# Moving the attention's weighted values one step later, next to the scores of another step

## The chip, the cores and the metric

The kernel runs on one core of a Trainium2 chip. The metric is the device time of one execution in microseconds. Five engines work at the same time, each on its own queue of instructions: PE (TensorE, matrix multiplies and transposes), DVE (VectorE), ACT (ScalarE), POOL (GpSimd) and SP (SyncE, which issues most of the DMAs). Instructions of different engines wait for each other on semaphores. PE writes its results to PSUM, which has eight banks; the other engines work mostly from SBUF.

## What is computed

Two layers run over a tensor x of 8 images, 256 channels and 64 x 64 points, all in float32. Layer 0 is an involution: 1x1 convolutions produce values and, through a small network, nine weights for each point and group of channels; each point gets the weighted sum of its nine neighbours. Layer 1 adds an attention over 7 x 7 neighbourhoods to a depthwise double convolution with weights computed at run time. The part that the change touches is the attention of layer 1:

```
att = einsum('bdn,bdkn->bnk', q, uk + upe[None])      # scores of a point against its 49 neighbours
att = softmax(att, axis=-1)                            # probabilities
out_att = einsum('bnk,bdkn->bdn', att, uv)             # weighted values
...
return rate1 * out_att + rate2 * out_conv
```

Both layers are residual: x = x + layer(groupnorm(x)).

## The kernel before

An image is cut into 8 bands of 8 rows; the 64 bands of layer 1 are numbered g, with b the image and i the band in it. One band of layer 1 takes 8 steps: `ct` (which 128 of the 256 channels, two heads of 64) times `m` (which 16 of the 64 columns). Layer 0 of a band 12 bands ahead runs beside layer 1, a piece in each step; in the last image nothing of layer 0 is left to run.

The order of the work on every engine is the order in which the program is written. A step is written out by hand in six parts, each of which ends with `advance()`. This call also runs whatever was put off by `after(n, f)`, n parts later. In a step of layer 1, in this order:

1. `scores` (L682): four matmuls of 64 x 64 tiles against 196 columns into the score tile `sco` (L692), a 14 x 14 window of keys for each of two 8 x 8 tiles of queries and two heads. VectorE adds the mask, writes the result to `prob`, and takes the negated maximum `nmax` of each row (L701). `transposed` (L720): PE transposes the probabilities of the step before (L724, tile `ptp`), and ScalarE copies them to SBUF as `pt` (L726). `exponentials`: ScalarE, with the row sums in `tot` (L709).
2. `branch_weights`: PE computes 512 columns of the convolution's dynamic weights (L814, tile `pf`), ScalarE takes their exponential into `ex` (L819). Two taps of the depthwise convolution on VectorE (L771 or L797).
3. `probabilities`: VectorE inverts `tot` (L716), ScalarE scales by it (L718). Then the work listed by `beside` for this step: queries (L625, copied out by ScalarE at L629), keys (L646, finished by VectorE at L654 and L661), values (L551), pieces of layer 0.
4. `weighted_values` (L729): eight products of `pt` with the values `vt` (L736, up to 112 rows, 64 columns of weights, 64 columns streamed), for the step before. They go to an unused part of the same score tile that this step's scores have filled. `add_values` (L744): VectorE adds the result to `xr`, the residual that is stored at the end of the band (L746). Then the remaining taps of this half.
5. The second `branch_weights` of the step; at the end of each `ct` the sum over the branches, on POOL and VectorE (`dynamic_sum`, L825 to L844).
6. More of the work beside: tap weights of layer 0 (L435, tile `pw`). VectorE multiplies them with the values (L448, tile `prod`) and POOL adds the products up (L456, tile `xg`), parts later.

PSUM is divided as follows. The score tile takes two banks and there is one such tile. So the scores of a step wait until VectorE has finished with everything in the tile of the step before. All other PE results (`pf`, `ptp`, `pw`, queries, keys, values) share five banks under the tag "gen". The accumulator of the depthwise convolution takes the last bank. In SBUF there are three `prob` tiles, two `pt` tiles and nine `vt` tiles.

Of the kernel before, what the change touches and what calls it, by code (L numbers as in the profile page):

```python
# [86 lines left out]
def conv_layers_kernel(ctx: ExitStack, tc: tile.TileContext, ins: dict, out: bass.AP):  # L87
# [98 lines left out]
    def layer1_loads():  # L186


        last = w1.tile([P, NCT, 1, C], F32, tag="rec", name="last", bufs=1)
        for f in late:  # L190
            f()
        nc.scalar.dma_start(out=last, in_=wfc_in[:, :, KK - 1 :])

        def first():
            nc.vector.tensor_scalar(wv, wv, rate1, None, ALU.mult)

        def difference(kt):
            nc.vector.tensor_sub(wfc[:, kt], wfc[:, kt], last[:, kt].to_broadcast([P, KK - 1, C]))  # L200

        return [first, lambda: difference(0), lambda: difference(1)]
# [12 lines left out]
    def after(n, f):  # L215
        later.append((place[0] + n, f))

    def advance():
        place[0] += 1
        ready = [f for p, f in later if p <= place[0]]  # L220
        later[:] = [d for d in later if d[0] > place[0]]
        for f in ready:
            f()
# [51 lines left out]
    def first_stats(b, i, use="xs", t=None, n=9):  # L275
        im = images[b]
        if i == 0:
            im.st0 = stat.tile([P, NCT, NB, 6], F32, tag="st", name=f"st0_{b}")
        x = load_x(b, i, use, t)

        def take():
            for ct in range(NCT):
                nc.vector.bn_stats(im.st0[:, ct, i, :], x[:, ct, :])

        after(n, take)
        return x
# [391 lines left out]
    def score_tile(nm):  # L678

        return ps.tile([P, 2, 512], F32, tag="sco", name=f"sco_{nm}")  # L680

    def scores(b, i, ct, m):  # L682


        im = images[b]
        qb, kb = im.qb[i, ct], im.kb[i, ct]
        nm = f"{b}_{i}_{ct}_{m}"
        sco = score_tile(nm)
        for t in range(2):
            for h in range(2):  # L690
                c0 = (2 * m + t) * TQ
                nc.tensor.matmul(  # L692
                    sco[half[t], h, :NKEY], qb[half[h], 2 * m + t].rearrange("p r c -> p (r c)"),
                    kb[half[h], :, c0 : c0 + KW], start=True, stop=True,
                )

        prob = probs[turn[0] % len(probs)]
        turn[0] += 1
        nmax = w1.tile([P, 2], F32, tag="nmax", name=f"nmax_{nm}", bufs=4)
        for h in range(2):  # L700
            nc.vector.tensor_tensor_reduce(  # L701
                prob[:, h, :NKEY], sco[:, h, :NKEY], mask, -1.0, 3.0e38, ALU.add, ALU.min, nmax[:, h : h + 1]
            )
        return sco, prob, nmax

    def exponentials(nm, prob, nmax):
        tot = w1.tile([P, 2], F32, tag="tot", name=f"tot_{nm}", bufs=4)
        for h in range(2):
            nc.scalar.activation(  # L709
                prob[:, h, :NKEY], prob[:, h, :NKEY], AF.Exp, bias=nmax[:, h : h + 1], scale=-1.0,  # L710
                accum_out=tot[:, h : h + 1],
            )
        return tot
# [6 lines left out]
    def transposed(nm, prob):  # L720
        ptp = ps.tile([CHUNK, 2, 2, P], F32, tag="gen", name=f"ptp_{nm}", bufs=5)
        for h in range(2):
            for ch in range(2):
                nc.tensor.transpose(ptp[:, h, ch], prob[:, h, ch * CHUNK : (ch + 1) * CHUNK], ident)  # L724
        pt = w1.tile([CHUNK, 2, 2, P], F32, tag="pt", name=f"pt_{nm}")
        nc.scalar.copy(pt, ptp)  # L726
        return pt

    def weighted_values(b, i, ct, m, pt, sco):  # L729
        im = images[b]  # L730
        po = sco[:, 0, 256 : 256 + 2 * NQ].rearrange("p (r c) -> p r c", r=R)
        for t in range(2):
            for ch in range(2):
                n = min(R, WP - (i + ch) * R) * KW
                for h in range(2):
                    nc.tensor.matmul(  # L736
                        po[half[h], :, t * TQ : (t + 1) * TQ],
                        im.vt[i + ch, m][:n, t, (2 * ct + h) * HD : (2 * ct + h + 1) * HD],
                        pt[:n, h, ch, t * NQ : (t + 1) * NQ],
                        start=(ch == 0), stop=(ch == 1),  # L740
                    )
        return po

    def add_values(b, i, ct, m, po):  # L744
        x = images[b].xr[i][:, ct].rearrange("p (r c) -> p r c", r=R)[:, :, 2 * m * TQ : 2 * (m + 1) * TQ]
        nc.vector.scalar_tensor_tensor(x, po, bv[:, ct : ct + 1], x, ALU.add, ALU.add)  # L746
# [203 lines left out]
    with tc.manual_schedule():  # L950

        for i, use in enumerate(("xc", "xc", "xr", "xr", "xs", None, None, None)):
            t = None
            if use is None:
                t = w1.tile([P, NCT, RP, W], F32, tag="yp", name=f"x_{i}", bufs=3)
                t = t.rearrange("p t r c -> p t (r c)")[:, :, :BAND]
            x = first_stats(0, i, use, t)
            if use == "xc":
                images[0].xc[i] = x
            advance()  # L960
        for r in range(NB, AHEAD0 - AHEAD):
            first_stats(*divmod(r, NB))
        for _ in range(10):
            advance()
        scaled_weights(0)
        for _ in range(32):
            advance()
        for n, f in enumerate(layer1_loads()):
            after(4 * STEPS * (3 + n), f)
        before = conv = None  # L970
        for g in range(-AHEAD, B * NB):
            b, i = divmod(g, NB)
            for s in range(STEPS):
                ct, m = divmod(s, NT // 2)
                mid, end = beside(g, s)
                steer(g, s)
                if g >= 0:
                    nm = f"{b}_{i}_{ct}_{m}"
                    sco, prob, nmax = scores(b, i, ct, m)
                    if before is not None:  # L980
                        pt = transposed(nm, before[-1])
                    tot = exponentials(nm, prob, nmax)
                advance()
                if g >= 0:
                    ex, exb = w1.tile([P, 2, BAND], F32, tag="ex", name=f"ex_{nm}", bufs=3), ex if m else None
                    branch_weights(b, i, ct, m, 0, ex)
                    if m in (0, 2):
                        todo = list(conv[0])
                    for _ in range(2):
                        todo.pop(0)()  # L990
                advance()
                if g >= 0:
                    probabilities(prob, tot)
                rest = [f() for f in mid]
                advance()
                if g >= 0:
                    if before is not None:
                        add_values(*before[:-1], weighted_values(*before[:-1], pt, sco))
                for f in rest:
                    if f:  # L1000
                        f()
                if g >= 0:
                    for _ in range(2 if m % 2 == 0 else len(todo)):
                        todo.pop(0)()
                    before = (b, i, ct, m, prob)
                advance()
                if g >= 0:
                    branch_weights(b, i, ct, m, 1, ex)
                    if exb is not None:
                        after(4, lambda ex=ex, exb=exb: nc.gpsimd.tensor_add(ex, ex, exb))  # L1010
                    if m == 1:
                        conv[1]()
                        conv = depthwise_middle(b, i, ct)
                    if m == NT // 2 - 1:
                        oc = depthwise_end(b, i, ct, conv[1])
                        after(4, lambda a=(b, i, ct, ex, oc): dynamic_sum(*a))
                if s % 4 == 3 and 0 <= (g * NCT + ct + 1) < B * NB * NCT:
                    gn, cn = divmod(g * NCT + ct + 1, NCT)
                    conv = depthwise_begin(*divmod(gn, NB), cn)
                advance()  # L1020
                for f in end:
                    f()
                advance()
        sco = score_tile("end")
        add_values(*before[:-1], weighted_values(*before[:-1], transposed("end", before[-1]), sco))
        for _ in range(40):
            advance()

# [81 lines left out]
```

The softmax here doesn't subtract the row's maximum and nothing guards it: scores larger than these inputs give would overflow.

## Time and profile before

| | before |
|---|---|
| time, median of 3 runs | 4332.86 us (4330.35 to 4334.35) |
| profiled span | 4333.4 us |
| start, before the first scores of layer 1 | 257.3 us |
| granted TensorE clock | 0.992 of full speed |
| scores L692, on PE | 4096 matmuls, mean 357 ns |
| weighted values L736, on PE | 8176 matmuls, mean 228 ns |
| additions L746, on VectorE | 511, mean 343 ns |
| dynamic weights L814, on PE | 4096 matmuls, mean 607 ns |

A float32 product appears in the trace as two matmuls. The duration of a matmul covers its way through the array, and consecutive ones overlap; what one costs the engine is therefore read from the distance between two starts, not from its duration. Small matmuls on different parts of the array run at the same time. In the profile "X <- Y" is an engine that sat idle ahead of its instruction X until Y released it, followed by the sum in microseconds, the number of times and the longest time. PEld is the weight load of TensorE, which overlaps matmuls.

### The profile page before, as it was taken

The page shows a single profiled execution, that of the slowest core. Times are in us where ns is not written, and L with a number is a line of the kernel's source. Part 1 is how long each engine was busy: PE and PEld are TensorE (multiplying, and loading weights), DVE is VectorE, ACT ScalarE, POOL GpSimd, SP SyncE. Part 2 cuts the span into 40 slices and gives each one's busy share as a digit, 9 for nine tenths or more (in the row PEclk, how much of TensorE's full clock was granted, in tenths as well). Part 3 has the DMA queues.
Part 4 walks back from the last instruction along what each step waited for, and adds up shares of the span by engine and source line. Part 5 has one row for each costly group of instructions (what it writes and reads, how often), then busy time and mean ns, then how long its engine had stood idle before and what let it go on. Part 6 is the DMA issues. An engine that isn't in the chain of part 4 may idle for free.

```text
span 4333.4 us, 72039 instructions
## 1 busy us (share of the span) xinstructions
PE 4174.8 (96%) x25004; PEld 2104.1 (49%) x25004; DVE 3577.6 (83%) x7244; ACT 3059.9 (71%) x7598; POOL 2900.3 (67%) x1778
## 2 busy tenths in 40 slices
PE   6789999999999999999999999999999999999998
PEld 3344445444454444544455444554445444454444
DVE  5778888888888888888888888888888888977777
ACT  3367777777777777877777777777677777677776
POOL 4657677676776767767776767766776777744445
PEclk9899999999999999999999999999999999999999
DMA  7754234234233333333333333343332232111100
GB/s 214 188 130 106 69 87 105 69 91 100 64 97 96 79 89 87 84 91 95 76 84 95 82 95 84 75 101 83 77 88 78 66 96 73 35 44 37 37 27 20
DMA packets 381259, 367.90 MB, mean 85 GB/s; under 512 B 55392, under 2 KB 282720, under 8 KB 380640
## 3 DMA queue, kind: packets, MB, share of 16 engines
q1 hardware_dynamic: 377568, 358.68, 32.6%
q8 instruction: 198, 3.24, 0.3%
q10 hardware_dynamic: 3328, 4.62, 0.3%
q14 instruction: 165, 1.35, 0.1%
HBM read 261.48 MB, written 101.71 MB: 84 GB/s over the span
## 4 chain that ended last, share of the span: by engine, by line
PE 61%; DVE 19%; POOL 11%; issue 5%; SPq 1%; DMA 1%; ACT 1%; POOLq 0%; ACTq 0%; DVEq 0%
PE pf L814 27%; POOL xg L456 6%; PE sco L736 5%; PE p L357 4%; PE pk L646 4%; DVE prod L448 4%; PE ptp L724 4%; PE sco L692 4%; DVE acc L771 3%; POOL ex L1010 3%; PE pq L625 3%; PE pvt L595 3%; DVE ex L832 2%; PE p L325 2%; DVE acc L797 2%
## 5 line engine op out<-in xcount | busy, mean ns | idle before, releaser
L814 PE MATMUL pf<-yp,c_wfc 128*128 128x512 f32 x4096 | 1985.1, 607 | 0.9
L456 POOL TENSOR_TENSOR xg<-xg,prod 128x1024 f32<-128x1024 f32 x549 | 1204.1, 2193 | 131.6 <-DVE prod L448 109.8
L1010 POOL TENSOR_TENSOR ex<-ex,ex 128x1024 f32<-128x1024 f32 x384 | 907.8, 2364 | 76.0 <-ACT ex L819 71.3
L814 PEld LDWEIGHTS pf<-yp,c_wfc 128*128 128x128 f32 x4096 | 696.2, 190 | 535.1 <-issue 491.0
L819 ACT ACTIVATE ex<-pf 128x512 f32<-128x512 f32 x1024 | 608.4, 594 | 453.6 <-PE pf L814 263.5
L842 POOL TENSOR_TENSOR ex<-ex,rec 128x512 f32<-128x512 f32 x128 | 163.7, 1279 | 1006.7 <-DVE rec L837 946.6
L771 DVE SCALAR_TENSOR_TENSOR acc<-yp,c_chan,acc 128x504 f32<-128x504 f32 (+3 forms) x1104 | 765.1, 693 | 55.4 <-ACT acc L762 35.0
L797 DVE SCALAR_TENSOR_TENSOR acc<-hid,c_chan,acc 128x504 f32<-128x504 f32 (+3 forms) x1024 | 758.0, 740 | 18.6 <-ACT acc L791 0.6
L448 DVE SCALAR_TENSOR_TENSOR prod<-pw,c_par,x3q 128x1040 f32<-128x1040 f32 x576 | 733.8, 1280 | 33.6 <-POOL xg L456 19.4
L718 ACT ACTIVATE prob<-prob,tot 128x196 f32<-128x196 f32 x1024 | 411.6, 451 | 427.6 <-DVE tot L716 427.6
L709 ACT ACTIVATE prob<-prob,nmax 128x196 f32<-128x196 f32 x1024 | 461.7, 455 | 85.7 <-DVE nmax L701 85.3
L736 PEld LDWEIGHTS sco<-pt,vt 112*64 112x64 f32 x8176 | 281.5, 137 | 363.5 <-issue 139.7
L701 DVE CUSTOM_DVE_ANT_0 prob<-sco,c_mask 128x196 f32<-128x196 f32 x1024 | 324.5, 355 | 159.8 <-PE sco L692 159.6
L746 DVE SCALAR_TENSOR_TENSOR xr<-sco,bv,xr 128x128 f32<-128x128 f32 x511 | 175.4, 343 | 334.5 <-PE sco L736 334.5
L736 PE MATMUL sco<-pt,vt 112*64 112x64 f32 x8176 | 350.2, 228 | 30.3 <-DVE nmax L701 28.4
L724 PE MATMUL ptp<-ident,prob 128*112 128x128 f32 x2044 | 331.6, 285 | 0.0
L726 ACT COPY pt<-ptp 112x512 f32<-112x512 f32 x511 | 296.3, 580 | 39.4 <-PE ptp L724 39.3
L692 PE MATMUL sco<-kb,qb 64*64 64x196 f32 x4096 | 294.7, 357 | 24.5 <-DVE xr L746 24.5
L724 PEld LDWEIGHTS ptp<-ident,prob 128*112 128x112 f32 x2044 | 206.4, 133 | 152.0 <-issue 66.0
L551 PE MATMUL pv<-yp,c_wv 128*128 128x512 f32 (+2 forms) x576 | 251.9, 562 | 0.0
L646 PE MATMUL pk<-yp,c_wk 128*128 128x512 f32 (+2 forms) x576 | 244.9, 552 | 0.0
L357 PE MATMUL p<-xc,w3s 128*128 128x512 f32 x512 | 243.7, 599 | 0.0
(133 smaller groups left out, 5359.2 us busy)
## 6 DMA issues: line engine op xcount, KB each, us to landing
x<-x3n SPq DMA_DIRECT2D x128, 264.0 KB, 2.1
x3q<-x SPq DMA_DIRECT2D x128, 264.0 KB, 7.1
xc<-in_x SPq DMA_DIRECT2D x64, 512.0 KB, 5.1
xg<-in_x SPq DMA_DIRECT2D x256, 128.0 KB, 4.8
x<-xg SPq DMA_DIRECT2D x256, 128.0 KB, 2.4
yp<-x SPq DMA_DIRECT2D x128, 256.0 KB, 3.3
xr<-x SPq DMA_DIRECT2D x64, 512.0 KB, 5.8
out_x<-xr SPq DMA_DIRECT2D x64, 512.0 KB, 3.1
```

The lines of the kernel that those rows point to most:

```text
L448: nc.vector.scalar_tensor_tensor(prod[:, :, :RUN], pw[:, j, :RUN].unsqueeze(1).to_broadcast([P, SHARE, RUN]), par[:, PCB2 + k : PCB2 + k + 1],
L456: nc.gpsimd.tensor_add(im.xg[i], im.xg[i], rows(prod))
L646: nc.tensor.matmul(pk[:, :n], wk[:, kt, ct * P : (ct + 1) * P], im.yp[i][:, kt, a : a + n], start=(kt == 0), stop=(kt == NCT - 1),)
L692: nc.tensor.matmul(sco[half[t], h, :NKEY], qb[half[h], 2 * m + t].rearrange("p r c -> p (r c)"), kb[half[h], :, c0 : c0 + KW], start=True, ...
L709: nc.scalar.activation(prob[:, h, :NKEY], prob[:, h, :NKEY], AF.Exp, bias=nmax[:, h : h + 1], scale=-1.0, accum_out=tot[:, h : h + 1],)
L724: nc.tensor.transpose(ptp[:, h, ch], prob[:, h, ch * CHUNK : (ch + 1) * CHUNK], ident)
L736: nc.tensor.matmul(po[half[h], :, t * TQ : (t + 1) * TQ], im.vt[i + ch, m][:n, t, (2 * ct + h) * HD : (2 * ct + h + 1) * HD], pt[:n, h, ch ...
L771: nc.vector.scalar_tensor_tensor(o, yp[:, ct, ra + dr : rb + dr, ca + dc : cb + dc], chan[:, ct, CW1 + k : CW1 + k + 1], o, ALU.mult, ALU.add,
L797: nc.vector.scalar_tensor_tensor(o, hid[:, ra + dr : rb + dr, ca + dc : cb + dc], chan[:, ct, CW2 + k : CW2 + k + 1], o, ALU.mult, ALU.add,)
L814: nc.tensor.matmul(pf, wfc[:, kt, 2 * m + j, ct * P : (ct + 1) * P], images[b].yp[i][:, kt, PAD : PAD + R], start=(kt == 0), stop=(kt == N ...
L819: nc.scalar.activation(ex[:, j].rearrange("p (r c) -> p r c", r=R), pf, AF.Exp)
L1010: after(4, lambda ex=ex, exb=exb: nc.gpsimd.tensor_add(ex, ex, exb))
```

## The change

The weighted values of a step are computed one step later than before. Before, the step that follows transposed the probabilities, and the weighted values came in mid-step, in the tile that held this following step's scores. Now they come at the very start of the step after that, as the first thing written to that step's score tile, right ahead of its scores. VectorE adds them right after it has taken the maxima of these scores, early in the step, where the addition stood in mid-step before. The purpose is to put the two kinds of small matmuls side by side on PE, and to have nothing in mid-step that occupies the score tile.

For this, `scores` gets its tile from the caller, and a list `pending` carries the transposed probabilities from one step to the next. At the end, two rounds instead of one finish the last two steps' weighted values.

```diff
-    def scores(b, i, ct, m):
+    def scores(b, i, ct, m, sco):
...
-        sco = score_tile(nm)
...
-        return sco, prob, nmax
+        return prob, nmax
...
-        before = conv = None
+
+        pending, before, conv = [], None, None
...
                 if g >= 0:
                     nm = f"{b}_{i}_{ct}_{m}"
-                    sco, prob, nmax = scores(b, i, ct, m)
-                    if before is not None:
-                        pt = transposed(nm, before[-1])
+                    sco = score_tile(nm)
+                    weighted = [(a, weighted_values(*a, pt, sco)) for a, pt in pending]
+                    prob, nmax = scores(b, i, ct, m, sco)
+                    for a, po in weighted:
+                        add_values(*a, po)
+                    pending = [] if before is None else [(before[:-1], transposed(nm, before[-1]))]
                     tot = exponentials(nm, prob, nmax)
...
                 rest = [f() for f in mid]
                 advance()
-                if g >= 0:
-                    if before is not None:
-                        add_values(*before[:-1], weighted_values(*before[:-1], pt, sco))
                 for f in rest:
...
-        sco = score_tile("end")
-        add_values(*before[:-1], weighted_values(*before[:-1], transposed("end", before[-1]), sco))
+        for last in (before, None):
+            sco = score_tile(f"end{last is None}")
+            weighted = [(a, weighted_values(*a, pt, sco)) for a, pt in pending]
+            for a, po in weighted:
+                add_values(*a, po)
+            pending = [] if last is None else [(last[:-1], transposed("end", last[-1]))]
```

## The prediction

> **What bounds the kernel now.** I read the page's busy shares first, then what TensorE waits for, then its order of work in one step, then the chain of waits through three steps.
>
> ```profile
> PE 4174.8 (96%) x25004; PEld 2104.1 (49%) x25004; DVE 3577.6 (83%) x7244; ACT 3059.9 (71%) x7598; POOL 2900.3 (67%) x1778
> PE 61%; DVE 19%; POOL 11%; issue 5%; SPq 1%; DMA 1%; ACT 1%; POOLq 0%; ACTq 0%; DVEq 0%
> PE sco L736 <- DVE nmax L701: 28.4, 62, 1.8
> PE sco L692 <- DVE xr L746: 24.5, 36, 2.0
> DVE xr L746 <- PE sco L736: 334.5, 306, 3.2
> ```
>
> PE is busy 96% of the span and carries 61% of the chain that ended last; DVE and POOL carry 30% of it. So PE is the bound most of the time, but not everywhere. PE's waits at the two groups that share the score tile are 28.4 + 24.5 = 53 us: weighted values wait for VectorE's maxima of the same tile, scores for the addition of the step before. The 334.5 us that VectorE waits for weighted values costs nothing by itself.
>
> "Busy" hides a second cost. PE's timeline around weighted values (start, duration; three narrow windows of one step):
>
> ```profile
> 2716.24 1.02 PE L551 MATMUL pv<-yp,c_wv 128*128 128x512 f32 x2
> ...
> 2716.67 0.59 PE L551 MATMUL pv<-yp,c_wv 128*128 128x512 f32 x1
> 2717.19 0.69 PE L736 MATMUL sco<-pt,vt 112*64 112x64 f32 x16
> ...
> 2717.81 1.12 PE L814 MATMUL pf<-yp,c_wfc 128*128 128x512 f32 x2
> ...
> 2718.34 1.45 PE L814 MATMUL pf<-yp,c_wfc 128*128 128x512 f32 x3
> ```
>
> Two 512-wide matmuls start 0.43 us apart (2716.24, 2716.67), but the first weighted one starts 0.52 after the last wide one, and behind the group the second wide one starts 0.53 after the first. Over all 512 steps, the trace's start times give these medians. Wide to wide: 429 ns. Wide to L736 or L692: 522, so 93 lost. Last L736 to wide: 151, where 64 columns take 53 elsewhere, so 98 lost. The second wide matmul behind it: 534, so 105 lost. L692 to the transposes L724: 98 lost, and 50 at the second transpose. Every change between tile shapes costs about 95 ns, whichever shapes they are, plus a refill.
>
> The chain through steps 4 to 6 of a typical band (start, duration, engine, group):
>
> ```profile
> 2714.31 1.22 DVE prod L448
> ...
> 2716.18 2.16 POOL xg L456
> 2718.34 2.33 POOL ex L1010
> ...
> 2720.74 1.28 POOL ex L825
> ...
> 2722.04 2.87 DVE ex L832
> ...
> 2724.93 1.75 DVE rec L833
> ```
>
> ```profile
> 2736.62 0.67 ACT L629 ACTIVATE qb<-pq,bq 128x512 f32<-128x512 f32 x1
> ...
> 2737.34 1.98 PE L814 MATMUL pf<-yp,c_wfc 128*128 128x512 f32 x4
> ```
>
> Here PE does not set the pace. A product of step 4 (it needs pw, PE's last work of step 3) feeds POOL; POOL's sum at L825 releases VectorE's L832, which takes 2.87 us; VectorE is then full up to the reciprocal of step 6 at 2735.71. ScalarE's probabilities and queries follow, ending at 2737.29; only then does PE get the PSUM buffer for pf of step 7, at 2737.34. From the end of probabilities to the first transpose of the next step I get medians of 4.5, 3.0, 1.3, 3.0, 2.3, -0.03, 0.18 and 0.87 us for steps 0 to 7 (the second half is needed about 0.27 later): ample at steps 0 to 4 and 7, none after 5 and 6.
>
> **What the Trainium skill says.** "TensorEngine Tiling (Array Packing)", section Key Properties: changing the tiling mode, not just the tile, drains TensorE. The trace agrees: 93 to 98 ns at each change. Weighted values use 64-column tiles over up to 112 rows, scores 64x64 tiles: by its list (section Tiling Modes) these are two modes, so the new neighbours do not merge. "TensorE: Matmul & The Clock Gate", Part 1, on queues: ScalarE and VectorE are strict first in, first out. The trace agrees: ScalarE stood 4.87 us for tot of step 5 while pv and pf lay finished behind it. "PSUM — Partial Sum Buffer", section on bank collisions: two engines may not touch one bank in the same partitions at once. That fits weighted values waiting for the maxima of another part of their bank (28.4 us); no run here shows a collision.
>
> **The change part by part.** No operation is added or removed, save an almost empty extra round at the very end. Matmuls (L736: 0.55 to 0.62 us a step), copies and additions (0.35 us) keep number and size.
>
> *PE's shape changes.* Before: into scores 93, into weighted values 93, out of them 98 + 105, together 389 ns a step; the way out to the transposes (98 + 50) stays. After: into weighted values 93, weighted values to scores U, and nothing in mid-step, since wide follows wide. The trace never shows L736 followed by L692. Lower end: U = 0 if the pair overlapped; upper end 145 (95 and a refill of 50). I take 95, as all other changes cost. Saved: 389 - 188 = 201 ns a step, over 511 steps 103 us (U = 0: 151; U = 145: 77).
>
> *PE's waits.* Weighted values now start on a tile whose last readers (maxima and addition) stood at the head of VectorE's previous step. Both waits, 53 us, go. Their input pt gets a whole step, so ScalarE's copy is never late. Behind the waiting weighted values now stand scores and transposes, but the wait should be over.
>
> *VectorE.* The addition stands behind the maxima, which wait for later matmuls than it needs, so it no longer blocks in mid-step. Scores come 0.62 us later in the step, but so do the next transposes, so that chain keeps its length, less the shorter step. The addition now stands ahead of tot: up to 0.3 us later where VectorE is full. In step 5 of the shown band maxima and addition should end near 2721.7 by the old clock, before POOL's release at 2722.0: hidden, by 0.3 us.
>
> *Buffers.* pt has two, enough. The values vt of an image's last band are read one step later, at seven boundaries: one wait of ScalarE for matmuls that come next in PE's queue, under 1 us each; nothing. The store of xr comes more than two steps after the last addition: nothing.
>
> *Where the saving counts.* In bands 0 to 5 of the first seven images, the chain from step 3's pw to step 7's pf runs over POOL, VectorE and ScalarE and keeps its length: savings in steps 4, 5 and 6 turn into PE waiting for probabilities at L724 and for the buffer at L814. So 5 of 8 steps count: 42 bands x 5 x 0.201 = 42 us. In bands 6 and 7 queries come a step earlier and the gate is looser (1.1 and 1.6 us of slack at step 7's transposes), so I count all steps: 14 x 1.6 = 22. The last image has no layer 0 beside it and PE is 100% busy there: 8 x 1.6 = 13. Sum 77. Of the 53 us of waits, the 24.5 at scores (nearly all in step 6) and about 10 of the others lie in the gated stretch and come back elsewhere; 18 stay won. For additions ahead of tot, and buffers running short in steps 0 to 3, I take off 10. Net 77 + 18 - 10 = 85 us: 4333 - 85 = 4248.
>
> **The rivals.**
> *A, PE alone is the bound.* Everything counts: 103 + 53 = 156, 4177 us. For it: PE's 96%, VectorE's 83%. Against: the chain shown, and no slack after steps 5 and 6.
> *B, the saving is mostly eaten.* U at its upper end (151 ns): 77/103 of 77 is 58; and the waits return in full, with 18 lost on late tot in steps 0 to 4: 58 - 18 = 40, 4293 us. For it: slack of 1.3 us at step 2 shrinks by 0.2 + 0.3. Against: it stays positive.
> *C, slower.* VectorE is the bound in all 56 bands, PE's saving there is worth nothing, maxima come 0.6 us later in step 5 and three additions of 0.27 stand before tot in steps 4 to 6: 56 x 1.4 = 79, less 13 in the last image, half of it hidden: about +35, 4368 us. For it: only 0.3 us of cover. Against: VectorE idles through most of steps 0 to 4, so lateness does not carry over.
> *D, no change.* A new buffer gate takes all 85 us: 4333.
>
> **How the numbers follow.** Main case 0.57, A 0.18, B 0.15, C 0.06, D 0.04. The time is the main case's, 4248. Low end 4175 takes in A; high end 4300 takes in B; C, D and an overlap of the two groups (U = 0 with A, about 4130) are left out. Faster 0.57 + 0.18 + 0.15 = 0.90, same 0.04, slower 0.06.
>
> **What would show it.** Right: PE's waits L736 <- nmax and L692 <- xr gone; wide to wide at 429 ns in mid-step; L736 to L692 about 150 ns start to start (53 + 95); new PE waits at L724 for ScalarE's probabilities and at L814 in steps 6 and 7; bands 0 to 5 about 1 us shorter and the last image's 1.6; VectorE waiting longer for scores at L701, less at L746. Wrong: L736 to L692 near 53 ns (U = 0) or above 200; PE waiting at L736 for VectorE's addition; L832 starting later after step 5's scores than POOL releases it (C); bands 0 to 5 shorter by the full 1.6 us and more (A).

## The result and the profile after

The changed kernel takes 4216.54 us (median of 4 runs, 4213.1 to 4219.91) against 4333.6 us before: 117 us less, a ratio of 0.9731 (95% interval 0.9714 to 0.9748). 4248 was forecast; the direction holds, and the gain is 117 instead of 85 us.

The page of the changed kernel: PE's share, and the engines of the chain that ended last. Lines from L683 on have moved up by one (L814 is now L813).

```profile
PE 4079.7 (97%) x25004; PEld 2134.8 (51%) x25004; DVE 3582.1 (85%) x7244; ACT 3046.5 (72%) x7598; POOL 2900.3 (69%) x1778
...
PE 74%; DVE 12%; POOL 7%; ACT 3%; issue 2%; SPq 2%; DMA 1%; POOLq 0%; ACTq 0%; DVEq 0%
```

PE now makes up 74% of the chain instead of 61%; DVE and POOL fell from 30% to 19%. PE's instructions are the same in number. What PE waits for in the changed kernel:

```profile
PE ptp L723 <- ACT prob L717: 25.9, 51, 2.7
PE ph L417 <- ACT hid L406: 17.4, 22, 1.5
...
PE pf L813 <- ACT vc L569: 4.3, 6, 0.7
...
PE sco L691 <- DVE kb L661: 0.2, 1, 0.2
```

The 28.4 us at weighted values and the 24.5 us at scores are gone. In their place stands a wait that was not there: the transposes L723 wait 25.9 us for ScalarE's probabilities. PE's timeline through the same steps (4 to 6, and the start of 7) of the same band as in the prediction, g = 37:

```profile
2636.86 0.84 PE L435 MATMUL pw<-h2n,c_c 128*128 128x132 f32 x6
2637.63 0.69 PE L735 MATMUL sco<-pt,vt 112*64 112x64 f32 x16
2638.24 0.57 PE L691 MATMUL sco<-kb,qb 64*64 64x196 f32 x8
...
2648.36 1.88 PE L551 MATMUL pv<-yp,c_wv 128*128 128x512 f32 x4
2650.08 1.88 PE L813 MATMUL pf<-yp,c_wfc 128*128 128x512 f32 x4
...
2652.56 0.69 PE L735 MATMUL sco<-pt,vt 112*64 112x64 f32 x16
2653.18 0.58 PE L691 MATMUL sco<-kb,qb 64*64 64x196 f32 x8
2654.12 0.78 PE L723 MATMUL ptp<-ident,prob 128*112 128x128 f32 x4 [0.36 <-ACT prob L717]
...
2660.42 0.69 PE L735 MATMUL sco<-pt,vt 112*64 112x64 f32 x16
2661.03 0.57 PE L691 MATMUL sco<-kb,qb 64*64 64x196 f32 x8
2661.94 0.78 PE L723 MATMUL ptp<-ident,prob 128*112 128x128 f32 x4 [0.34 <-ACT prob L717]
2662.87 1.55 PE L813 MATMUL pf<-yp,c_wfc 128*128 128x512 f32 x3
```

Two things are to be seen. In mid-step, wide follows wide without a seam (the time that PE loses where the tile shape changes): four pv take 1.72 us (2648.36 to 2650.08), 0.43 each. And the three small groups stand together at the start of a step, where PE waits: ahead of the transposes of steps 6 and 7, and ahead of the first pf of step 7. From the last tap weights of step 3 (L435) to that pf the kernel before took 2737.34 - 2711.35 = 25.99 us, the changed one 2662.87 - 2636.86 = 26.01. The chain of waits over this stretch, changed kernel, names what sets it:

```profile
2646.20 1.28 POOL ex L824
...
2647.51 2.86 DVE ex L831
...
2653.51 0.08 DVE tot L715
...
2653.61 0.47 ACT prob L717
...
2654.12 0.78 PE ptp L723 x4
...
2661.33 0.08 DVE tot L715
...
2661.43 0.81 ACT prob L717 x2
2662.24 0.58 ACT qb L629
...
2662.87 1.55 PE pf L813 x3
```

POOL's sum, VectorE's L831 of 2.86 us, the reciprocals, ScalarE's probabilities and queries, then PE. The gate of the prediction (the stretch in which other engines set PE's pace) is there. That it is as long as before does not show this by itself, as the part on the prediction works out.

The bands, from the first scores of one to the first scores of the next (start times in the two traces), mean over images. The two bands of image 6 that are set apart, 4 and 5, won only 0.34 and 0.08 us; why was not settled.

| bands | gain each, us | sum, us |
|---|---|---|
| 0, 1, 2, 4, 5 of the first seven images | 1.51 (1.58 without two bands of image 6) | 52.7 |
| 3 of these images | 2.40 | 16.8 |
| 6 and 7 of these images | 2.14 and 2.53 | 32.7 |
| last image, seven of its bands | 1.59 | 11.1 |

With 3.2 us ahead of the first scores (257.3 and 254.1 us), where nothing was changed, and 1.6 in the last band this makes the 118.1 us between the two profiled spans (4333.4 and 4215.3). The 3.2 us need not belong to the change: ahead of the first scores the profiled executions of all kernels range from 250.5 to 257.3 us.

### The profile page after: what moved, and what is told of

It is laid out like the page before. It is cut to its first block, busy times and chain, and to the rows that moved or that the text cites. A ratio compares the mean times of both kernels' runs of the same rounds, so it can differ in the third digit from the quotient of the medians.

```text
span 4215.3 us, 72044 instructions
## 1 busy us (share of the span) xinstructions
PE 4079.7 (97%) x25004; PEld 2134.8 (51%) x25004; DVE 3582.1 (85%) x7244; ACT 3046.5 (72%) x7598; POOL 2900.3 (69%) x1778
## 4 chain that ended last, share of the span: by engine, by line
PE 74%; DVE 12%; POOL 7%; ACT 3%; issue 2%; SPq 2%; DMA 1%; POOLq 0%; ACTq 0%; DVEq 0%
PE pf L813 34%; PE ptp L723 6%; PE sco L735 5%; PE pk L646 5%; PE sco L691 5%; PE p L357 4%; POOL xg L456 4%; DVE prod L448 4%; PE pq L625 3%; PE pv L551 3%; PE pvt L595 2%; PE p L325 2%; PE pw L435 2%; POOL ex L1010 2%; DVE acc L796 2%
## 5 line engine op out<-in xcount | busy, mean ns | idle before, releaser
L813 PE MATMUL pf<-yp,c_wfc 128*128 128x512 f32 x4096 | 1932.4, 595 | 9.3 <-ACT vc L569 4.3
L456 POOL TENSOR_TENSOR xg<-xg,prod 128x1024 f32<-128x1024 f32 x549 | 1203.4, 2192 | 127.4 <-DVE prod L448 104.4
L813 PEld LDWEIGHTS pf<-yp,c_wfc 128*128 128x128 f32 x4096 | 733.8, 191 | 702.7 <-issue 658.9
L700 DVE CUSTOM_DVE_ANT_0 prob<-sco,c_mask 128x196 f32<-128x196 f32 x1024 | 325.1, 355 | 292.5 <-PE sco L691 292.0
L708 ACT ACTIVATE prob<-prob,nmax 128x196 f32<-128x196 f32 x1024 | 462.2, 456 | 46.9 <-DVE nmax L700 46.4
L735 PEld LDWEIGHTS sco<-pt,vt 112*64 112x64 f32 x8160 | 279.2, 137 | 209.5 <-issue 71.4
L723 PE MATMUL ptp<-ident,prob 128*112 128x128 f32 x2044 | 341.3, 287 | 26.4 <-ACT prob L717 25.9
L735 PE MATMUL sco<-pt,vt 112*64 112x64 f32 x8160 | 349.7, 228 | 0.0
L723 PEld LDWEIGHTS ptp<-ident,prob 128*112 128x112 f32 x2044 | 204.1, 133 | 194.0 <-ACT prob L717 69.4
L691 PE MATMUL sco<-kb,qb 64*64 64x196 f32 x4096 | 294.5, 357 | 0.2 <-DVE kb L661 0.2
L625 PE MATMUL pq<-yp,c_wq 128*128 128x512 f32 x512 | 242.2, 596 | 2.3 <-DVE prod L448 2.3
```

The source lines that it names most:

```text
L456: nc.gpsimd.tensor_add(im.xg[i], im.xg[i], rows(prod))
L691: nc.tensor.matmul(sco[half[t], h, :NKEY], qb[half[h], 2 * m + t].rearrange("p r c -> p (r c)"), kb[half[h], :, c0 : c0 + KW], start=True, ...
L708: nc.scalar.activation(prob[:, h, :NKEY], prob[:, h, :NKEY], AF.Exp, bias=nmax[:, h : h + 1], scale=-1.0, accum_out=tot[:, h : h + 1],)
L735: nc.tensor.matmul(po[half[h], :, t * TQ : (t + 1) * TQ], im.vt[i + ch, m][:n, t, (2 * ct + h) * HD : (2 * ct + h + 1) * HD], pt[:n, h, ch ...
L813: nc.tensor.matmul(pf, wfc[:, kt, 2 * m + j, ct * P : (ct + 1) * P], images[b].yp[i][:, kt, PAD : PAD + R], start=(kt == 0), stop=(kt == N ...
```

## The experiments

Theory: PE sets the time except in the gated stretch from step 3's tap weights to step 7's pf, in bands with layer 0 beside them. Rivals are named with each run. All kernels ran beside the kernel before, which took 4332.3 to 4333.0 us (medians).

**The lag alone.** All weighted values one step later, but back in mid-step.

```diff
-                    weighted = [(a, weighted_values(*a, pt, sco)) for a, pt in pending]
+                    here = True
+                    weighted = [] if here else [(a, weighted_values(*a, pt, sco)) for a, pt in pending]
...
+                    held = pending if here else []
...
                 advance()
+                if g >= 0:
+                    for a, pt in held:
+                        add_values(*a, weighted_values(*a, pt, sco))
```

> The weighted values come one step later, as in the changed kernel, but stay in mid-step where they were before, with their addition behind them; the transposed probabilities have a whole step. My theory: the lag alone is worth next to nothing, since the changes of tile shape (389 ns a step) and both waits on the score tile are those of before; only ScalarE's late copies (1.9 us in all) go. Expected 4325 to 4335 us, waits at weighted values and at scores about 28 and 25 us. Rival (the extra step of slack for the transposed probabilities is what pays): 4260 or less.

4331.92 us, ratio 0.9995 (0.9987 to 1.0004). PE's waits in this run:

```profile
PE sco L691 <- DVE xr L745: 24.5, 37, 2.0
...
PE sco L735 <- DVE nmax L700: 21.6, 53, 1.7
```

The gain comes from where the group and its addition stand; the step of slack alone is worth nothing.

**The addition late.** The changed kernel, only VectorE's addition back in mid-step.

```diff
-                    for a, po in weighted:
-                        add_values(*a, po)
...
                 advance()
+                if g >= 0:
+                    for a, po in weighted:
+                        add_values(*a, po)
```

> The changed kernel with only VectorE's addition put back into mid-step; matmuls stay next to the scores. My theory: weighted values of step 6 then wait for the addition of step 5, which stands behind the reciprocal of step 5, about 0.9 us; but PE would wait there for probabilities and the queries' buffer anyway, so the total moves little: 4208 to 4228 us. Rival (the early release of the score tile is a main source of the gain): the 24.5 us of waits for the addition come back in full, 4240 us or more.

4236.99 us, 20.5 more than the changed kernel: between the two expectations, nearer to the rival's. PE's longest wait is now

```profile
PE sco L735 <- DVE xr L745: 64.4, 98, 3.0
```

and the wait for probabilities has left the list. So the gate did absorb most of this wait, but not all: bands 1 to 5 of the first six images became 0.22 to 0.29 us longer. In band 1 PE starts the first pf of step 6 0.8 us later and wins only part of that back up to step 7. In the last image, where no gate stands, bands 1 to 6 became 0.29 us longer too, by a wait for the addition at the start of step 2. With the matmuls where they are, the early addition is worth 20 us. I had taken it for nearly free.

**Extra PE work in step 1 or step 5.** One more matmul of 256 columns, in `branch_weights`; the diff is that of step 1, the kernel for step 5 has (1, 1, 0).

```diff
+        if (ct, m, j) == (0, 1, 0):
+            nc.tensor.matmul(
+                pf[:, : R // 2], wfc[:, 0, 2 * m, ct * P : (ct + 1) * P],
+                images[b].yp[i][:, 0, PAD : PAD + R // 2], start=True, stop=True,
+            )
```

> The changed kernel with one extra matmul of 256 columns (two in the trace, 0.43 us) in step 1 of every band, overwritten by the one behind it; the output is unchanged. Both theories: PE sets the pace in step 1, so it costs 64 x 0.43 = 27 us: 4244 us.

> The same extra matmul in step 5 instead of step 1. My theory: in bands 0 to 5 with layer 0 beside them the chain over POOL, VectorE and ScalarE sets the time from step 3's tap weights to step 7's pf, so the matmul runs in time that PE would wait; only bands 6, 7 and the last image pay: 4 to 11 us, 4220 to 4228 us. Rival (PE alone is the bound, its remaining waits are scattered): 27 us as in step 1, 4244 us.

Step 1: 4244.63 us, 28.1 more. Step 5: 4223.38 us, 6.8 more. In the trace of step 1's kernel nearly every band is 0.40 to 0.46 us longer. In that of step 5's, bands 1 to 4 of the first seven images differ by 0.03 us at most, band 6 and those of the last image pay 0.41 to 0.46. PE's wait for probabilities gave the room:

```profile
PE ptp L723 <- ACT prob L717: 12.1, 23, 2.2
```

12.1 us in step 5's kernel, 25.9 without the extra matmul. In the band g = 37 the stretch from step 3's tap weights to step 7's pf takes 25.97 us with the extra matmul in it and 26.01 without. This shows the gated stretch directly: the same work costs its full time in one step and nothing in another.

**One step's weighted values back in mid-step.** As in the first experiment, for a single step of each band: step 7 in the diff, step 1 (`s == 1`) in the second kernel.

```diff
+                    here = s == 7
-                    weighted = [(a, weighted_values(*a, pt, sco)) for a, pt in pending]
+                    weighted = [] if here else [(a, weighted_values(*a, pt, sco)) for a, pt in pending]
...
+                    held = pending if here else []
...
                 advance()
+                if g >= 0:
+                    for a, pt in held:
+                        add_values(*a, weighted_values(*a, pt, sco))
```

> The changed kernel with the weighted values (and their addition) put back into mid-step in step 7 of every band alone. My theory: at the start of step 7 PE waits for probabilities and for the queries' buffer, so the weighted group there runs in waiting time; in mid-step, behind the first pf, it falls into the part that PE sets: 0.55 us of matmuls and 0.2 us of shape changes in some 42 bands, 0.2 us in the other 22: 42 x 0.75 + 22 x 0.2 = 36 us, 4252 us (4244 to 4260). Rival (only the number of shape changes counts): 64 x 0.2 = 13 us, 4229 us.

> The same in step 1 of every band alone. Both theories: PE sets the pace there on both sides of the move, so only the shape changes count: 64 x 0.2 = 13 us, 4229 us (4224 to 4234).

Step 7: 4263.43 us, 46.9 more. Step 1: 4240.27 us, 23.7 more. Both lie above what was expected, by some 11 us, and the traces say where. In step 7's kernel bands 1 to 5 are 0.78 to 0.85 us longer (0.75 expected, one band of image 6 aside) and those of the last image 0.20 (0.2 expected). Bands 6 and 7 of the first six images add 1.3 and about 0.37 instead of 0.2, with a wait at weighted values for the maxima in each (8.6 us, 12 times, of which 6.3 us in band 6). In step 1's kernel most bands are 0.16 to 0.22 us longer, but band 7 of the first six images 1.6, with new waits at value tiles for keys (4.4 us, 6 times), which are about half of what these bands lost too much. Why they come there was not settled. The point in dispute is clear in the bands without such waits: the move costs 0.2 us where PE sets the pace on both sides of it, and 0.8 where it crosses the end of the gate. In the band g = 37 the stretch takes 26.01 us with the group of step 7 taken out of it, as long as with the group in it. The room that it left stood empty; waits of PE in step 7's kernel:

```profile
PE ptp L723 <- ACT prob L717: 48.0, 51, 2.7
```

**Loosening the gate.** First the work beside ahead of the probabilities; then VectorE's part of the sum over the branches behind tot.

```diff
+                rest = [f() for f in mid]
                 if g >= 0:
                     probabilities(prob, tot)
-                rest = [f() for f in mid]
```

> The changed kernel with the list of work beside (queries, keys, values and what ScalarE copies out of them) ahead of the inversion of tot and the scaling of the probabilities, instead of behind. ScalarE then empties the queries' buffer of step 6 while it waits for tot. My theory: the 17 us that PE waits at pf in steps 6 and 7 go: about 4200 us (4195 to 4210); the waits at the transposes stay. Rival (this gate only hides another one behind it): no change, 4212 to 4220 us.

```diff
-            after(3, second)
+            after(2, second)
...
-            after(2, weigh)
+            after(1, weigh)
...
-        after(5, quotient)
+        after(7, quotient)
```

> The changed kernel with VectorE's part of the sum over the branches (L831 and the first reciprocal behind it) two parts later, behind tot of step 5 instead of ahead of it; the second reciprocal and POOL's products stay where they were. My theory: tot of step 5 comes 4 to 5 us earlier and the wait at the transposes of step 6 goes (16 us), the one of step 7 only if L831 no longer runs beside POOL (0.42 instead of 2.85 us): 4165 to 4200 us. Rival (VectorE's total load in steps 5 to 7 is what counts, wherever the sum stands): 4210 to 4220 us.

4201.66 us and 4175.1 us: 14.9 and 41.4 less than the changed kernel, both in the range that the theory gave. The second edit does not leave the second reciprocal where it was, as the expectation says: it comes 7 + 2 parts after the sum is begun, where it came 5 + 3. In this kernel bands 1, 2 and 4 lose another 1.0 us, and steps 6 and 7 take 7.29 us each where they took 7.4 and 8.2. In most bands of the last image, where PE is always busy, these steps take 7.29 us as well, so in these bands PE sets the pace again. VectorE's timeline in step 5 of the same band g = 37, in the kernel with the late quotient:

```profile
2624.37 0.16 DVE L715 RECIPROCAL tot<-tot 128x2 f32<-128x2 f32 x1
2624.44 1.71 DVE L831 TENSOR_SCALAR ex<-ex 128x512 f32<-128x512 f32 x1
```

and in the changed kernel:

```profile
2647.51 2.85 DVE L831 TENSOR_SCALAR ex<-ex 128x512 f32<-128x512 f32 x1 [0.30 <-POOL ex L824]
2650.39 1.75 DVE L832 RECIPROCAL rec<-ex 128x256 f32<-128x256 f32 x1
2652.06 1.45 DVE L770 SCALAR_TENSOR_TENSOR acc<-yp,c_chan,acc 128x504 f32<-128x504 f32 x2
2653.41 0.16 DVE L715 RECIPROCAL tot<-tot 128x2 f32<-128x2 f32 x1
```

The reciprocal that ScalarE's probabilities need now stands ahead of L831. It starts 2.9 us after the step's first scores (those start at 2621.46), against 7.8 us in the changed kernel (2653.41 - 2645.65). L831 became shorter too, which was not intended: 1.71 us here, and 100.5 instead of 137.2 us in all (the last section shows on what its length depends). So not all of the 41 us need come from the new order alone. The wait for probabilities is down from 25.9 to

```profile
PE ptp L723 <- ACT prob L717: 8.2, 15, 1.6
```

**The gate loosened on both bases.** The kernel before with the same three delays, and the changed kernel with both edits.

> The kernel before the change with VectorE's part of the sum over the branches two parts later, as in e8. My theory: with the chain over L832 out of the way the change is worth what PE saves, 103 us of shape changes, and the waits that are then left at the score tile. In the kernel before, the waits in steps 5 and 6 (27 us at scores, about 20 at weighted values) shrink by half or more: 4285 to 4310 us, so that the change is worth 110 to 135 us on this base (against 4175). Rival (the gate does not limit the kernel before, since its mid-step waits are what delays it): 4325 to 4335 us, and the change is worth 150 to 160 us, all that the first estimate for PE alone gave.

> e7 and e8 together on the changed kernel: work beside ahead of the probabilities, and VectorE's part of the sum two parts later. My theory: e8 has already removed most of what e7 removes (6 us of waits at pf are left of 17), so the two do not add up: 4165 to 4178 us. Rival (independent gates): 4160 us or less. If copies now wait in front of the probabilities where these have become the last to be ready, slower than e8.

4282.48 us and 4168.13 us; the first lies just below the 4285 to 4310 us expected. With the late quotient in both, the change is worth 4282.5 - 4175.1 = 107 us, against 117 without it. That is a little under the 110 to 135 of the theory and far under the rival's 150 to 160: the edit frees the kernel before by about as much as the changed one (about 51 and 41 us). In bands 1, 2 and 4 steps 6 and 7 now take 7.49 us each in the old order and 7.29 in the new one, and the change wins 0.20 us in each of the eight steps, about 1.58 a band (band 4 of image 6 aside): what it won there with the gate in place. Of the waits at scores almost nothing is left on the old base; 19.3 us at weighted values remain:

```profile
PE sco L736 <- DVE nmax L701: 19.3, 21, 1.8
```

The two loosenings do not add up: 7 us instead of 15 on top. The last kernel is the fastest of all, 0.9619 of the time before (0.9605 to 0.9634).

## Why the prediction was right, and where it was off

*Shape changes: right.* From the last L735 to the first L691 it is 151 ns on average (150 to 153), 53 of streaming and 98 of seam: U is 98, taken as 95. "TensorEngine Tiling (Array Packing)", section Key Properties, holds for this pair too: two small modes side by side still drain. Mid-step seams are gone. The last image, where nothing else binds, won 1.59 us a band where 8 x 0.201 = 1.6 was forecast.

*Waits at the score tile: right that they go and mostly come back.* 18 us less 10 for late tot was forecast to stay won, 8 us. If every band had won the 1.59 us of the last image, that would make 102 of the 115 us behind the first scores; the other 13 are waits that did not come back, in bands 3, 6 and 7. Late tot did no visible harm in steps 0 to 4, which lose 0.20 us each in band 1, the shape changes alone. That the addition is worth 20 us by itself was not seen.

*The gate: right that it stands, wrong in what it takes from the gain.* The waits moved to L723 and L813 as forecast, and VectorE's wait for scores grew from 159.6 to 292.0 us. But the forecast named "about 1 us" for bands 0 to 5 as a sign of being right and "the full 1.6 us and more" as a sign for rival A, that PE alone is the bound. Bands 0, 1, 2, 4 and 5 won 1.58, within 0.02 us of that sign, and band 3 more. Neither this nor the length of the stretch tells the two apart. PE's own work in the stretch hardly changed: the seams of steps 4, 5 and 6 fell by 0.20 us each, 0.60 in all, and a fourth group of 0.55 to 0.62 us came in. So PE alone would have kept the length too. That other engines set it is shown by the extra matmul in step 5, by the group taken out of step 7, and by the late quotient. Rival A (4177 us) was nearly right in its sum for the shape changes, 103 us (102 measured), and wrong in the waits, of which 13 and not 53 us stayed won. The measured 4216.5 lies about halfway between the forecast and this rival, so the total alone would not decide between them.

*Where the saving counts: the term that was mis-sized.* "5 of 8 steps count: 42 bands x 5 x 0.201 = 42 us" was too low. It counts the shape changes on PE's side of the gate, but not where the group itself has moved. The stretch begins at the last tap weights of step 3 and ends at the first pf of step 7. Before, the mid-step groups of steps 4, 5 and 6 lay in it: three. After, the groups at the start of steps 4, 5, 6 and 7: four. One whole group, 0.55 us or a little more, went from time that PE sets to time in which PE waits. 1.0 + 0.55 comes close to the 1.58 us that these bands won; in 42 bands it makes 23 of the 32 us that were missing. The pair of kernels with one step's group moved back shows it: 0.2 us where the move does not cross the gate's end, 0.8 where it does. That what crosses the gate's end nearly equals what three gated steps lose is a coincidence of this kernel; it makes the gate take nothing from the shape changes here. Of the other 9 us, about 5 are the waits (13 instead of 8), and 3.2 lie ahead of the first scores and need not belong to the change.

*Slower or no change: fell.* The maxima and the addition of step 5 end at 2647.2, POOL's release comes at 2647.5: the forecast cover of 0.3 us is there.

## What to carry to other kernels

Put groups of small matmuls of unlike shapes next to each other and leave wide ones beside wide ones: in these traces each seam on PE costs about 0.1 us, and the wide matmuls behind it another 0.1. Where a chain of other engines gates PE, ask not only which waits a change removes but on which side of the gate its work ends up: work that moves into the waiting time is free as far as the wait reaches. An unchanged length of a gated stretch proves nothing until PE's own work in it has been added up. A cheap test of where a bound lies is a small extra matmul, once in a step that should pay for it and once in one that should not.

## What was not expected of the hardware

VectorE's L831 is the same instruction 128 times (128x512, in place) and takes 0.41 to 2.87 us. Those of the second half of the channels (`ct` = 1) have a median of 0.42 us, those of the first 2.37. The one in the gated stretch starts 0.08 us behind POOL's 2.18 us addition L456 (2647.43) and takes 2.85. With the quotient two parts later, L831's sum falls from 137.2 to 100.5 us and VectorE's busy time from 3582 to 3535. The traces show on what the length depends. In the changed kernel 54 of the 128 start while an instruction of POOL runs, and every one of them ends 0.28 to 0.29 us after POOL's instruction has ended (where a second one follows at once, after that one); the other 74 take 0.41 to 0.43. With the late quotient 48 start 0.08 to 1.80 us into POOL's instruction, and again all end 0.28 to 0.29 us behind it. So this instruction of VectorE, when it starts beside one of POOL, lasts until POOL is done. Why it does so, no run here shows.
